# Perceiver layer on one core: the order of the first loads, keys, latents and maxima

## The chip, the cores and the metric

The kernel runs on one core of a Trainium2 chip. The metric is the device time of one execution in microseconds, as the median of several runs on the chip. The engines are TensorE (PE, with its weight loads shown apart as PEld), VectorE (DVE), ScalarE (ACT), GpSimd (POOL) and SyncE (SP); SP, ACT and POOL also issue DMAs, each through its own queue.

## What is computed

One layer with three residual blocks on latents x of 4 batches x 256 rows x 256: cross attention to a context of 4096 rows per batch, causal linear attention over the latents, and a gated feed-forward block. All is in float32. The change lies in the start of the first block:

```python
def _L0_xattn_ref(query, key, value, Wq, bq, Wk, bk, Wv, bv, Wh, bh):
    Q = query @ Wq.T + bq
    K = key @ Wk.T + bk
    V = value @ Wv.T + bv
    ...
    dot = jnp.einsum('bhsd,bhtd->bhst', Q, K) / np.sqrt(D_HEAD)
    scores = jax.nn.softmax(dot, axis=-1)
    out = jnp.einsum('bhst,bhtd->bhsd', scores, V)
    return out @ Wh.T + bh

x = x + _L0_xattn_ref(_layernorm(x), ctx_1024, ctx_1024, Wq, bq, Wk, bk, Wv, bv, Wh, bh)   # 16 heads of 16
x = x + _L0_attn_ref(_layernorm(x), ...)
x = x + _L0_ffn_ref(_layernorm(x), ...)
```

## The kernel before

**Tiling.** Cross attention runs in 16 units u, each one batch and four heads (`NU`), and each unit in 16 steps of 256 context rows (`NS`). A unit needs the keys of its heads for all 4096 context rows in one of three key buffers `kts`, and the largest score of each query row and head before its exponentials. The maxima of unit u + 1 are therefore made during the steps of unit u. The context comes in eight chunks of 512 rows (`NCH`), four chunk buffers (`cpool`), each chunk loaded by SP.

**Keys** (`key`, L630). For a chunk, 16 matmuls in two halves (tile `pk`), each evicted by ScalarE with the bias `bk_sb` into `ku` (L650), and after the second half eight DMAs (L653) that bring each head's rows into `kts`. For chunk 0 of the first batch the DMAs are issued by SP and ScalarE in turn, for all others by SP alone. The bias `bk_sb` is filled by sixteen small DMAs that GpSimd issues at the very start (L74), eight for each of its two columns. The weights arrive as `wk` and are copied without their padding to `wk_sb` (L883), on ScalarE.

**Latents and queries** (`queries`, L830). For a batch: `layernorm` (L96) in three pieces, statistics on VectorE, the root on ScalarE (L109), scaling on VectorE (L114); `turn`, which transposes on TensorE (L160) and copies to `zT` on ScalarE (L161); and `project`, queries of two head groups (tile `pq`, L848), evicted by ScalarE with the bias `bq_sb` into `qT` (L853).

**Maxima** (`maxima`, L694). For a unit and step, four matmuls of 128 queries by 512 keys (tile `pm`, L708), and one reduction each on VectorE (L715). When a unit's are complete, `shift` reduces them to `neg` (L722), transposes that on TensorE (`pn`, L727) and adds it to the queries (`qa`, L731), from which the main loop's scores (L745) are made.

**Order.** Inside `manual_schedule` (L861) TensorE, ScalarE, VectorE and SP do their work in the order in which the program is written; nothing overtakes on an engine. All PSUM tiles come from one pool of eight banks (`bank`, L179). The prologue of the first unit is written out by hand: loads, first keys, first queries, then sixteen groups g. In each group the four products of step g's maxima, a piece of the normalisation of batches 2 and 3 if one is due (`parts`), the reductions, and then one piece of `fill_in`: the keys of a chunk, the queries of a later batch (with `turn` in the piece where they are first wanted), or the values of a chunk. After groups 4, 6, 8 and 12 ScalarE fills a quarter of the third key buffer (`filled`, L906). After the groups named in `extra` come two groups of maxima of unit 1, ahead of its turn. Then the main loop begins, in which two units' work is interleaved until the causal attention and the feed-forward block follow.

Its core in the code:

```python
            for g, piece in enumerate(fill_in):
                products, reduce = maxima(g, range(4))
                products()
                if g in parts:
                    parts[g]()
                reduce()
                ...
                piece()
                ...
                if g in extra:
                    products, reduce = maxima(NS + extra[g], range(4))
```

Of the kernel before, what the change touches and what calls it, by code (L numbers as in the profile page):

```python
# [12 lines left out]
F32 = mybir.dt.float32  # L13
# [7 lines left out]
P = 128  # L21
B, T, D = 4, 256, 256
S = 4096
H, HD = 16, 16
KC = D // P
NT = B * T // P
NQ = H // 4
# [12 lines left out]
def perceiver_layer(  # L40
# [5 lines left out]
    nc = tc.nc  # L46
    const = ctx.enter_context(tc.tile_pool(name="const", bufs=1))

    def load(src, shape, name, dtype=F32, queue=None, pool=const):
        t = pool.tile(shape, dtype, tag=name, name=name)  # L50
        (queue or nc.scalar).dma_start(out=t, in_=src)
        return t


    xr = const.tile([P, NT, D], F32, tag="xr", name="xr")

    def load_x(b):
        nc.sync.dma_start(
            out=xr[:, 2 * b : 2 * b + 2, :],
            in_=x[b * T : (b + 1) * T, :].rearrange("(t p) d -> p t d", p=P),  # L60
        )

    load_x(0)
    eps = const.tile([P, 1], F32, tag="eps", name="eps")
    nc.gpsimd.memset(eps, LN_EPS)
    ident = const.tile([P, P], F32, tag="ident", name="ident")
    make_identity(nc, ident)
    wq_sb = load(wqP, [P, KC, NQ * P], "wq_sb")
    bq_sb = load(bqP, [P, NQ], "bq_sb")
    bk_sb = const.tile([P, KC], F32, tag="bk_sb", name="bk_sb")  # L70
    for q in range(NQ):
        for j in range(4):
            h = 4 * (q % 2) + j
            nc.gpsimd.dma_start(  # L74
                out=bk_sb[h * HD : (h + 1) * HD, q // 2 : q // 2 + 1],
                in_=bkP[32 * j + 1 : 32 * j + 1 + HD, q : q + 1],
# [208 lines left out]
    def start_causal():  # L285
# [75 lines left out]
        return norms, [call(lambda pieces: [piece() for piece in pieces], pieces) for pieces in others]  # L361

    finish = cross_attention(
        tc, xr, load_x, load_rest, ctxT, wq_sb, bq_sb, wkP, bk_sb, wvP, eps, ident, layernorm, transposed,
        qT, kts, lnp, bank, rest, start_causal)
    wout_sb = rest[8]

# [6 lines left out]
    for i in (0, 2):  # L374
        nc.gpsimd.affine_select(
            out=mask[:, i, :], in_=mask[:, i, :], compare_op=ALU.is_ge, fill=0.0, base=0,
# [189 lines left out]
                piece()  # L566


def cross_attention(tc, xr, load_x, load_rest, ctxT, wq_sb, bq_sb, wkP, bk_sb, wvP, eps,
                    ident, layernorm, transposed, qT, kts, lnp, bank, rest, start_causal):  # L570


# [14 lines left out]
    nc = tc.nc  # L587
# [4 lines left out]
    with ExitStack() as st:  # L592
# [10 lines left out]
        wk_sb = big.tile([P, KC, D], F32, tag="wk_sb", name="wk_sb")  # L603
        wv_sb = big.tile([P, KC, D], F32, tag="wv_sb", name="wv_sb")
        wide = st.enter_context(tc.tile_pool(name="wide", bufs=1))
        wk = wide.tile([P, KC, H, 32], F32, tag="wk", name="wk")
# [13 lines left out]
        def load_context():  # L620
            for _, p, c in itertools.islice(loads, 1):
                t = cpool.tile([P, KC, CH], F32, tag="ctx", name="ctx")
                nc.sync.dma_start(out=t, in_=ctxT[p // 2, c])
                contexts.append(t)

        def context(p, c):
            load_context()
            return contexts.pop(0)

        def key(p, c, queues=(nc.sync, nc.sync)):  # L630

            m, x = p % 2, context(p, c)
            ku = upool.tile([P, CH], F32, tag="ku", name="ku")
            made = []

            def half(part):
                pk = bank([P, CH // 2], "pk")
                made.append(pk)
                cs = slice(part * (CH // 2), (part + 1) * (CH // 2))
                for k in range(KC):  # L640
                    for j in range(4):
                        nc.tensor.matmul(  # L642
                            pk[32 * j : 32 * j + 32, :],
                            lhsT=wk_sb[:, k, m * P + 32 * j : m * P + 32 * j + 32], rhs=x[:, k, cs],
                            start=k == 0, stop=k == KC - 1,
                        )

            def out(part):
                cs = slice(part * (CH // 2), (part + 1) * (CH // 2))
                nc.scalar.activation(ku[:, cs], made.pop(), AF.Identity, bias=bk_sb[:, m : m + 1])  # L650
                for h in range(8 if part == 1 else 0):
                    r0 = 32 * (h % 4) + 1
                    queues[h % 2].dma_start(  # L653
                        out=kts[(2 * p + h // 4) % 3][r0 : r0 + HD, c * CH : (c + 1) * CH],
                        in_=ku[h * HD : (h + 1) * HD, :],
                    )

            return half, out
# [27 lines left out]
        def whole(item):  # L686
            half, out = item
            for part in range(2):
                half(part)
                out(part)  # L690
# [139 lines left out]
        def queries(b):  # L830

            z = lnp.tile([P, 2, D], F32, tag="z1", name="z1", bufs=4)
            got = []

            def norm():
                return layernorm(lambda t: z[:, t % 2, :], (2 * b, 2 * b + 1))

            def turn():
                zT = lnp.tile([P, KC, T], F32, tag="zT1", name="zT1")
                got.append(zT)  # L840
                for i in range(2):
                    transposed(zT[:, :, i * P : (i + 1) * P], z[:, i, :])

            def project(q):
                ps = bank([P, 2, T], "pq")
                for i in range(2):
                    for k in range(KC):
                        nc.tensor.matmul(  # L848
                            ps[:, i, :], lhsT=wq_sb[:, k, (q + i) * P : (q + i + 1) * P],
                            rhs=got[0][:, k, :], start=k == 0, stop=k == KC - 1,  # L850
                        )
                for i in range(2):
                    nc.scalar.activation(  # L853
                        qT[:, q + i, b * T : (b + 1) * T], ps[:, i, :], AF.Identity,
                        bias=bq_sb[:, q + i : q + i + 1],
                    )

            return norm, turn, project

        both = (nc.sync, nc.scalar)  # L860
        with tc.manual_schedule(engines={ET.PE, ET.Activation, ET.DVE, ET.SP}):  # L861
            nc.sync.dma_start(out=wk, in_=wkP.rearrange("p k (h r) -> p k h r", r=32))
            for b in range(1, B):
                load_context()
                load_x(b)
            nc.sync.dma_start(out=wv, in_=wvP)

# [5 lines left out]
            def fill(kt, c0, c1, engine=nc.vector):  # L873
                engine.tensor_copy(kt[:, c0 * CH : c1 * CH], ones.to_broadcast([P, (c1 - c0) * CH]))

            qs = [queries(b) for b in range(B)]
            for i in range(2):
                fill(kts[i], 0, 2)
            normal = [q[0]() for q in qs]
            for piece in normal[0]:  # L880
                piece()
            for k in range(KC):
                nc.scalar.copy(  # L883
                    wk_sb[:, k, :].rearrange("p (h d) -> p h d", d=HD), wk[:, k, :, 1 : 1 + HD]
                )
            qs[0][1]()
            whole(key(0, 0, both))
            qs[0][2](0)
            whole(key(0, 1))
            for i in range(2):  # L890
# [18 lines left out]
            def keys(c):  # L909
                return lambda: whole(key(0, c))  # L910

            def values(c):
                return lambda: whole(value(0, c))

            def turned(b, c):
                def piece():
                    qs[b][1]()
                    qs[b][2](2 * c)

                return piece  # L920

            def queried(b, c):
                return lambda: qs[b][2](2 * c)

            fill_in = [
                keys(3), keys(4), turned(1, 0), queried(1, 1), keys(5), turned(2, 0), keys(6), queried(2, 1),
                keys(7), turned(3, 0), values(0), queried(3, 1), values(1), queried(0, 1), values(2), values(3),
            ]

            parts = dict(zip((1, 2, 3, 6, 7, 8), (*normal[2], *normal[3])))  # L930
            extra = {10: 0, 13: 1}
            for g, piece in enumerate(fill_in):
                products, reduce = maxima(g, range(4))
                products()
# [20 lines left out]
            for n in range(NU * NS + 1):  # L955
# [14 lines left out]
                if i < len(items) - NCH:  # L970
                    if half == 0:
                        what, p, c = items[i + NCH]
# [96 lines left out]
```

## Time and profile before

| what | value |
|---|---|
| median of 3 runs | 1228.5 us (1228.21 to 1228.61) |
| the profiled execution | 1229.02 us, span 1227.3 us |
| TensorE busy | 1193.0 us, 97% of the span |
| VectorE busy | 927.9 us, 76% |
| ScalarE busy | 673.0 us, 55% |
| GpSimd busy | 60.2 us, 5% |
| DMA, 2 to 14 us of the span | about 400 GB/s |
| GpSimd's bias DMAs, issue to landing | 2.8 to 6.9 us, median 5.0 |

The span is the time from the first to the last instruction of the profiled execution; the device time has some 1.7 us around it. A profile line of a timeline gives the start, the length, the engine, the program line, the operation with the tile it writes and the tile it reads, the count of merged instructions, and in brackets how long the engine was idle before it and what ended that. A float32 matmul appears as two records. TensorE's busy share counts time in which a matmul waits for its bank, so that a stretched group of matmuls, not a gap, is how a wait for PSUM looks.

### The profile page before, as it was taken

The page shows a single profiled execution, that of the slowest core. Times are in us where ns is not written, and L with a number is a line of the kernel's source. Part 1 is how long each engine was busy: PE and PEld are TensorE (multiplying, and loading weights), DVE is VectorE, ACT ScalarE, POOL GpSimd, SP SyncE. Part 2 cuts the span into 40 slices and gives each one's busy share as a digit, 9 for nine tenths or more (in the row PEclk, how much of TensorE's full clock was granted, in tenths as well). Part 3 has the DMA queues.
Part 4 walks back from the last instruction along what each step waited for, and adds up shares of the span by engine and source line. Part 5 has one row for each costly group of instructions (what it writes and reads, how often), then busy time and mean ns, then how long its engine had stood idle before and what let it go on. Part 6 is the DMA issues. An engine that isn't in the chain of part 4 may idle for free.

```text
span 1227.3 us, 42096 instructions
## 1 busy us (share of the span) xinstructions
PE 1193.0 (97%) x17712; PEld 807.0 (66%) x17712; DVE 927.9 (76%) x1823; ACT 673.0 (55%) x1394; POOL 60.2 (5%) x115
## 2 busy tenths in 40 slices
PE   7999999999999999999999999999999999959998
PEld 3566667666766676667666776677667755536777
DVE  6887777777777777777777777777788877577763
ACT  3456665566666655666656556655566546641311
POOL 4010000000000000000000000000001012120100
PEclk9999999999999999999999999999999999999999
DMA  6452331233123322332233213322232000020000
GB/s 208 135 192 67 101 114 56 80 105 106 64 79 89 116 71 63 103 119 72 60 102 106 86 58 91 103 90 73 86 105 91 5 1 4 2 80 1 10 9 18
DMA packets 57756, 95.78 MB, mean 78 GB/s; under 512 B 29024, under 2 KB 31712, under 8 KB 57568
## 3 DMA queue, kind: packets, MB, share of 16 engines
q1 hardware_dynamic: 56640, 92.44, 24.3%
q8 instruction: 140, 2.29, 0.8%
q10 hardware_dynamic: 416, 0.66, 0.2%
q14 instruction: 48, 0.39, 0.1%
q0 software_dynamic: 512, 0.00, 0.0%
HBM read 74.17 MB, written 1.05 MB: 61 GB/s over the span
## 4 chain that ended last, share of the span: by engine, by line
PE 92%; DVE 4%; ACT 1%; DMA 1%; issue 1%; SPq 0%; POOL 0%; DVEq 0%; ACTq 0%
PE pt L745 22%; PE pm L708 18%; PE pav L765 18%; PE pk L642 11%; PE pv L672 10%; PE pd L504 2%; PE pg L492 1%; PE pu L492 1%; PE pq L848 1%; PE pqk L211 1%; PE po L430 1%; PE pa L411 1%; PE py L823 1%; PE py L466 1%; DVE mx L715 1%; PE pf L275 1%
## 5 line engine op out<-in xcount | busy, mean ns | idle before, releaser
L715 DVE TENSOR_REDUCE mx<-pm 128x1 f32<-128x512 f32 x1024 | 635.6, 684 | 145.4 <-PE pm L708 145.3
L750 ACT ACTIVATE e<-pt 128x512 f32<-128x512 f32 x1024 | 529.2, 602 | 384.2 <-PE pm L708 359.6
L745 PE MATMUL pt<-qa,kt 32*128 32x256 f32 x4096 | 500.2, 388 | 1.3 <-DVE av L775 0.7
L708 PE MATMUL pm<-kt,qT 32*128 32x512 f32 x2048 | 494.6, 616 | 0.0
L745 PEld LDWEIGHTS pt<-qa,kt 32*128 32x128 f32 x4096 | 317.0, 184 | 117.2 <-ACT v L679 43.2
L765 PE MATMUL pav<-e,v 128*32 128x256 f32 x4096 | 269.8, 380 | 0.0
L708 PEld LDWEIGHTS pm<-kt,qT 32*128 32x128 f32 x2048 | 172.2, 184 | 15.5 <-issue 3.7
L765 PEld LDWEIGHTS pav<-e,v 128*32 128x32 f32 x4096 | 128.7, 110 | 73.9 <-ACT e L750 4.7
L775 DVE TENSOR_TENSOR av<-pav,av 128x256 f32<-128x256 f32 x240 | 101.7, 424 | 65.7 <-PE pav L765 65.4
L672 PE MATMUL pv<-wv_sb,ctx 128*32 128x128 f32 x4096 | 137.5, 276 | 0.0
L642 PE MATMUL pk<-ctx,wk_sb 128*32 128x256 f32 x2048 | 136.7, 388 | 0.0
L672 PEld LDWEIGHTS pv<-wv_sb,ctx 128*32 128x32 f32 x4096 | 104.2, 109 | 43.5 <-DVE mx L715 42.7
L642 PEld LDWEIGHTS pk<-ctx,wk_sb 128*32 128x32 f32 x2048 | 54.8, 110 | 67.1 <-DVE mx L715 39.0
L650 ACT ACTIVATE ku<-pk,bk_sb 128x256 f32<-128x256 f32 x128 | 63.2, 495 | 11.2 <-PE pk L642 9.9
L679 ACT COPY v<-pv 128x256 f32<-128x256 f32 x128 | 51.4, 402 | 9.9 <-PE pv L672 9.9
L802 POOL TENSOR_TENSOR on<-on,bv_sb 128x64 f32<-128x64 f32 x32 | 9.2, 308 | 820.5 <-DVE on L797 820.5
L421 DVE TENSOR_TENSOR at<-pa,mask 128x384 f32<-128x384 f32 x64 | 31.2, 550 | 7.0 <-PE pa L416 7.0
L282 ACT ACTIVATE kt<-kt,shift 128x512 f32<-128x512 f32 x32 | 22.4, 725 | 22.0 <-DVE kt L281 22.0
L281 DVE TENSOR_SCALAR kt<-pf,low,top 128x512 f32<-128x512 f32 x32 | 23.7, 803 | 3.9 <-PE pf L275 3.9
L492 PE MATMUL pg<-zT,wg 128*128 128x256 f32 x96 | 23.0, 382 | 0.7 <-ACT zT L484 0.7
L496 ACT ACTIVATE th<-pg 128x512 f32<-128x512 f32 x12 | 7.1, 594 | 29.8 <-PE pg L492 29.8
L492 PE MATMUL pu<-zT,wu 128*128 128x256 f32 x96 | 22.7, 379 | 0.0
(126 smaller groups left out, 565.6 us busy)
## 6 DMA issues: line engine op xcount, KB each, us to landing
ctx<-in_ctxT_dram SPq DMA_DIRECT2D x128, 512.0 KB
kt<-ku SPq DMA_DIRECT2D x508, 32.0 KB
xo<-on SPq DMA_DIRECT2D x128, 8.0 KB
xr<-in_x_dram SPq DMA_DIRECT2D x4, 256.0 KB
out_dram<-o SPq DMA_DIRECT2D x8, 128.0 KB
wqkv_sb<-in_wqkv_dram SPq DMA_DIRECT2D x1, 768.0 KB
w_i<-in_w_gate_dram SPq DMA_DIRECT2D x1, 768.0 KB
w_i<-in_w_up_dram SPq DMA_DIRECT2D x1, 768.0 KB
```

The source lines that it names most:

```text
L421: nc.vector.tensor_tensor(at, pa, mask, ALU.mult)
L492: nc.tensor.matmul(ps[:, i, :], lhsT=w[:, k, ns], rhs=zT[:, k, :], start=k == 0, stop=k == KC - 1)
L642: nc.tensor.matmul(pk[32 * j : 32 * j + 32, :], lhsT=wk_sb[:, k, m * P + 32 * j : m * P + 32 * j + 32], rhs=x[:, k, cs], start=k == 0, sto ...
L650: nc.scalar.activation(ku[:, cs], made.pop(), AF.Identity, bias=bk_sb[:, m : m + 1])
L672: nc.tensor.matmul(pv[32 * j : 32 * j + 32, i, :], lhsT=x[:, k, t0 + 32 * j : t0 + 32 * j + 32], rhs=wv_sb[:, k, m * P : (m + 1) * P], sta ...
L679: nc.scalar.copy(to.rearrange("p t (h d) -> p t h d", d=HD + 1)[:, :, :, :HD], made.pop().rearrange("p t (h d) -> p t h d", d=HD),)
L708: nc.tensor.matmul(pm, lhsT=qT[rows, q, t0 : t0 + P], rhs=kt[rows, c * CH : (c + 1) * CH], start=True, stop=True,)
L715: nc.vector.tensor_reduce(mx[:, i, j, c : c + 1], pm, AX.X, ALU.max)
L745: nc.tensor.matmul(pt[:, i, :], lhsT=kt[rows, ks], rhs=qa[rows, :], start=True, stop=True)
L750: nc.scalar.activation(e, pt, AF.Exp, scale=0.25)
L765: nc.tensor.matmul(pav[32 * h : 32 * h + 32, :], lhsT=v[:, t % KT, c0 : c0 + 32], rhs=es[n, h][:, i, :], start=i == 0, stop=i == 1,)
L775: nc.vector.tensor_tensor(avs[u], pav, avs[u], ALU.add)
```

## The change

The first load of the latents no longer stands at the head of the program; `wq_sb` is only allocated there, and both are loaded by SP behind the key weights and the first context chunk. One of the two copies to `wk_sb` goes to VectorE. The keys of chunk 0 are made before the first normalisation. `turned`, which transposed a batch's latents and projected them in the same piece, becomes `ahead`, which puts the transposition behind the keys of an earlier piece; the projections stay where they were. The two groups of unit 1's maxima move from behind groups 10 and 13 to behind groups 4 and 9.

```diff
-    load_x(0)
     eps = const.tile([P, 1], F32, tag="eps", name="eps")
...
-    wq_sb = load(wqP, [P, KC, NQ * P], "wq_sb")
+    wq_sb = const.tile([P, KC, NQ * P], F32, tag="wq_sb", name="wq_sb")
     bq_sb = load(bqP, [P, NQ], "bq_sb")
...
             nc.sync.dma_start(out=wk, in_=wkP.rearrange("p k (h r) -> p k h r", r=32))
+            load_context()
+            load_x(0)
+            nc.sync.dma_start(out=wq_sb, in_=wqP)
             for b in range(1, B):
-                load_context()
+                if b < B - 1:
+                    load_context()
                 load_x(b)
             nc.sync.dma_start(out=wv, in_=wvP)
...
             for i in range(2):
                 fill(kts[i], 0, 2)
+            for k, copy in enumerate((nc.scalar.copy, nc.vector.tensor_copy)):
+                copy(wk_sb[:, k, :].rearrange("p (h d) -> p h d", d=HD), wk[:, k, :, 1 : 1 + HD])
+            whole(key(0, 0, both))
             normal = [q[0]() for q in qs]
             for piece in normal[0]:
                 piece()
-            for k in range(KC):
-                nc.scalar.copy(
-                    wk_sb[:, k, :].rearrange("p (h d) -> p h d", d=HD), wk[:, k, :, 1 : 1 + HD]
-                )
             qs[0][1]()
-            whole(key(0, 0, both))
             qs[0][2](0)
             whole(key(0, 1))
...
-            def turned(b, c):
-                def piece():
-                    qs[b][1]()
-                    qs[b][2](2 * c)
-
-                return piece
+            def ahead(piece, b):
+
+                return lambda: (piece(), qs[b][1]())
...
             fill_in = [
-                keys(3), keys(4), turned(1, 0), queried(1, 1), keys(5), turned(2, 0), keys(6), queried(2, 1),
-                keys(7), turned(3, 0), values(0), queried(3, 1), values(1), queried(0, 1), values(2), values(3),
+                keys(3), ahead(keys(4), 1), queried(1, 0), queried(1, 1), ahead(keys(5), 2), queried(2, 0),
+                keys(6), queried(2, 1), ahead(keys(7), 3), queried(3, 0), values(0), queried(3, 1),
+                values(1), queried(0, 1), values(2), values(3),
             ]

             parts = dict(zip((1, 2, 3, 6, 7, 8), (*normal[2], *normal[3])))
-            extra = {10: 0, 13: 1}
+            extra = {4: 0, 9: 1}
```

More of the change, by code (lines that the diff above doesn't have):

```diff
@@ L363, in perceiver_layer @@
     finish = cross_attention(
-        tc, xr, load_x, load_rest, ctxT, wq_sb, bq_sb, wkP, bk_sb, wvP, eps, ident, layernorm, transposed,
+        tc, xr, load_x, load_rest, ctxT, wqP, wq_sb, bq_sb, wkP, bk_sb, wvP, eps, ident, layernorm, transposed,
         qT, kts, lnp, bank, rest, start_causal)
@@ L566, in perceiver_layer, with cross_attention @@
                 piece()
-def cross_attention(tc, xr, load_x, load_rest, ctxT, wq_sb, bq_sb, wkP, bk_sb, wvP, eps,
+def cross_attention(tc, xr, load_x, load_rest, ctxT, wqP, wq_sb, bq_sb, wkP, bk_sb, wvP, eps,
                     ident, layernorm, transposed, qT, kts, lnp, bank, rest, start_causal):
```

## The prediction

> **What bounds the kernel now.** I read the page first: its chain of what ended last gives the kernel to TensorE. So any microsecond by which TensorE reaches its main loop later, or sooner, should show in full at the end.
>
> ```profile
> PE 92%; DVE 4%; ACT 1%; DMA 1%; issue 1%; SPq 0%; POOL 0%; DVEq 0%; ACTq 0%
> ```
>
> The change lies in the first 75 us, so I read the chain in order of time there (start, length, what), which gives the milestones to compare with.
>
> ```profile
> 0.81 4.59 DMA xr<-in_x_dram
> ...
> 7.71 1.09 PE tr L160 x4
> 8.80 3.38 PE pk L642 x32
> 12.19 1.93 PE pq L848 x8
> 14.11 3.59 PE pk L642 x64
> 17.70 1.07 PE pm L708 x8
> ...
> 65.37 7.26 DVE mx L715 x12
> 72.65 0.23 DVE neg L722
> 73.02 0.42 PE pn L727 x2
> ```
>
> Latents land first, TensorE starts at 7.71 us, the first group of maxima starts at 17.63 us (the timeline's start of that pm) and the last transposition before the main loop at 73.02. Note that the first keys take 3.38 us, the next two pieces together 3.59.
>
> Then the timeline of the first 32 us (start, length, engine, line; in brackets the idle time before and who ended it).
>
> ```profile
> 1.39 0.70 POOL L74 DMA_DIRECT2D bk_sb<-in_bkP_dram  x1 [0.35 <-issue]
> 2.44 3.61 POOL L74 DMA_DIRECT2D bk_sb<-in_bkP_dram  x7
> 6.62 0.30 ACT L109 ACTIVATE ln_rs<-ln_mv,eps 128x2 f32<-128x2 f32 x1 [3.31 <-DVE ln_mv L106]
> 10.73 0.47 ACT L650 ACTIVATE ku<-pk,bk_sb 128x256 f32<-128x256 f32 x1 [1.52 <-PE pk L642]
> 12.27 0.47 ACT L650 ACTIVATE ku<-pk,bk_sb 128x256 f32<-128x256 f32 x1 [1.06 <-PE pk L642]
> 12.77 2.50 ACTq L653 DMA_DIRECT2D kt<-ku  x4
> 15.38 0.84 ACT L853 ACTIVATE qT<-pq,bq_sb 128x256 f32<-128x256 f32 x2 [2.64 <-DMA kt<-ku]
> ```
>
> Two things to see. ScalarE issues half of the first keys' DMAs and does nothing else for 2.50 us: the queries, done at 14.1, are evicted only at 15.38. And the keys' bias bk_sb comes over GpSimd's queue: the first eight of sixteen transfers (column 0, all that the first keys read) are issued by 6.05; the eighth, from about 5.58, lands 4.9 us later (the DMA view), at 10.5. GpSimd's ninth issue starts 0.3 us after the landing it waits for, so a waiter would go at about 10.75. The first eviction started at 10.73, 0.30 us after its products' last issue (8.73 + half of 3.39 = 10.43); the second, which has its bias, 0.15 after its own (12.12). So the bias is just in time now.
>
> Last the loop's timeline.
>
> ```profile
> 55.09 9.72 DVE L715 TENSOR_REDUCE mx<-pm 128x1 f32<-128x512 f32 x16 [0.47 <-PE pm L708]
> 57.78 1.56 PE L708 MATMUL pm<-kt,qT 32*128 32x512 f32 x8
> 68.12 2.08 PE L708 MATMUL pm<-kt,qT 32*128 32x512 f32 x8
> ```
>
> A pm group (x8) normally takes 1.07; these two take 1.50 and 2.02. All PSUM tiles share eight banks in turn. Group 12's fourth pm is the eighth tile after group 11's first, which VectorE frees with its fifth reduction: 55.09 + 5 x 0.605 = 58.12; it can start at 58.21, and 58.21 + 1.07 = 59.28 is where the next matmul starts. Group 15: 65.35 + 6 x 0.605 + 0.09 = 69.07, + 1.07 = 70.14, again the trace's number. So I can tell by hand where TensorE will wait for a bank.
>
> [...] 0.43 us per four matmuls of the first keys against 0.23 later, full speed from 12.1, 4.4 us after the start. [...]
>
> **The change, the front.** Loads: wk, context 0, latents 0, wq, now all on SP's queue, where the latents led and wq ran on ScalarE's. By the DMA view 0.51 MB had moved by 4.0 us, 1.02 by 5.25, 1.31 by 6.0; the latents' 0.26 MB were in at 4.72 and used at 5.42, 0.70 later. So: wk (0.52 MB) usable at 4.7, its two copies, now one each on ScalarE and VectorE (0.40 each), done at 5.1; context at 6.0; latents at 6.7; wq at 8.0. TensorE starts the first keys at 6.0, cold as before: halves done at 7.7 and 9.4. That is 2.7 us earlier than now. SP issues the latents third instead of first and wq besides (0.44 to 0.5 us each, all four out by 2.8): hidden behind the 400 GB/s that set the landings; with ScalarE one issue short, its table load comes 0.5 earlier, into idle time. VectorE's wk copy fits between its fills (done 4.05) and the latents (6.7).
>
> But program order now puts on ScalarE: both evictions, four DMA issues, and only then the root of the first normalisation, without which there are no latents to transpose. The bias transfers do not move (same queue, same traffic): column 0 still lands at 10.5. So
>
> - evictions from 10.73, two in 0.84: done 11.57
> - four issues, 2.50 plus the gaps of now: root at 14.21
> - root to first transposition, as now 6.62 to 7.71: 15.30
> - transpositions and zT copies, cold: now 7.71 to 9.21, plus 0.07: queries from 16.87 (warm, as at 24.64 to 25.81: 16.5)
> - queries 1.93, keys 1 and 2 3.59: 22.4
>
> TensorE is idle from 9.4 to 15.3, 5.9 us. [...] Costed from both sides: no cold phase, first group at 16.5 + 5.52 = 22.0[...]. I take the 4.4 us of now, cold to 19.7: half of 19.7 - 16.87 is lost, 1.42, so the first maxima start at 23.8. **Front: 23.8 - 17.63 = +6.2 us.** VectorE's fills, memsets and second normalisation come behind this root too: from 15.7, 3.4 + 1.3 + 1.2 to 21.8, its root on ScalarE behind key 1's evictions (22.6), scaling done at 23.9. The first reduction is due at 24.96, so that cover holds by 1 us; gone, it would cost what it lacks. SP's key DMAs (8 x 0.69) start just as long before their group as now.
>
> **The loop.** Removed: three waits for zT between transposition and queries (24.70 + 0.38 to 25.81: 0.73 each, 2.2 us), as the transposition now sits one group ahead, with a pm group to hide the copy. Moved: two groups of unit 1's maxima (1.07 us TensorE, 2.42 VectorE each) from behind groups 10 and 13 to behind 4 and 9. There VectorE already has the four normalisation parts (1.08 and 0.92 twice each) and little slack. From the first group's start as zero, with pm 1.07, keys 1.87, queries 1.93, values 1.89, transposition 0.45, reductions 0.605 from 1.16 behind their group, I follow both engines and the eight banks:
>
> - group 2, ready 6.33: its fourth bank is group 1's fourth, reduced late since normalisation 2 precedes it: 7.15. Wait 0.82
> - extra group at 16.54 behind group 4: bank at 16.82. Wait 0.28
> - group 7, ready 23.83: bank of group 6's second, 24.92. Wait 1.09
> - group 9, ready 31.31: bank 31.89. Wait 0.58
> - group 11, ready 38.92: bank 39.77. Wait 0.85
> - group 15 starts at 51.69, its reductions clean of backlog, so the last transposition comes 1.15 + 2.48 + 0.40 = 4.03 later, at 55.72
>
> Now it is 73.02 - 17.63 = 55.39. The zT waits (2.2), the present bank waits (0.43 + 0.95) and their knock-on go; 3.6 us of new bank waits come. **Loop: +0.3 us.** Moving queued maxima and dropping the stall buys nothing: the late backlog of VectorE becomes an early one.
>
> Sum +6.5 us on the profiled execution's 1229.0 (span 1227.3 and 1.7 around it): 1235.5. The runs' median is 0.5 below that execution: **1235.0**, 0.5% slower.
>
> **Rivals.**
> - Clock stays up across the gap: front +4.4, total +4.7: 1233.2. Against it 5.9 us of idling.
> - The bias lands by 7.6: evictions follow the products (done 10.0), root 12.65, idle 4.3 and still cold: first group at 22.25, total +4.9: 1233.4. Late bias transfers landed in 3 to 3.8 us, but with less traffic.
> - Banks don't hold (the reading of eight in turn is wrong at the new places): loop -3.3, total +2.9: 1231.4. Against it two places reckoned to 0.01 us.
> - Not slower: ScalarE reaches the root early. Place: its queue between first eviction and root; price 4.2 us of the front. If the bias is there and the four issues cost ScalarE nothing, root at 10.05, queries at 12.3[...]: first group at 17.85, total +0.5: 1229.0. It decides from a root before about 10.5. Without the bank waits on top 1225.4, faster. The trace's 2.64 us wait speaks against it.
>
> **Numbers.** Chances: forecast 0.45, warm clock 0.17, early bias 0.13, no bank waits 0.13, early root 0.12 (0.05 of it with the second piece). A measurement of this kernel tells 0.2%, 2.5 us, from no change: slower above 1231.0. The no-bank-waits case lies near the bound, 0.05 of it under: slower 0.83, same 0.12, faster 0.05. Range 1231.0 to 1236.8: [...] the forecast's own range is 1234.3 to 1236.4.
>
> **What would show it.** Right: first keys on TensorE at about 6, first eviction near 10.7 with idle ScalarE before it, root near 14.2, transpositions near 15.3, no matmul from 9.4 until then, queries over 3 us long; first maxima at 22 to 25; stretched pm groups at 2, 7, 9 and 11. Wrong: a root near 10, a first group before 20, or a loop under 53 us.

## The result and the profile after

The changed kernel takes 1234.66 us in the median (1233.92 to 1235.62, 4 runs) beside 1228.55 before (1228.21 to 1228.62): a ratio of 1.0051, 95% interval 1.0033 to 1.0068. It is slower by 0.5%, 6.1 us; 1235.0 was forecast. One execution each of e5, e10 and e11 below took at least 275 us longer than the others of its kernel, and these three are not in the ratios.

The chain by engine of the changed kernel's page is again TensorE's, over a longer span.

```profile
span 1232.2 us, 42099 instructions
...
PE 92%; DVE 4%; DMA 1%; ACT 1%; issue 1%; SPq 0%; POOL 0%; ACTq 0%; DVEq 0%
```

Its timeline of the first 40 us, the columns as before (start, length, engine, line, what; idle before it and by whom ended):

```profile
5.95 3.64 PE L641 MATMUL pk<-ctx,wk_sb 128*32 128x256 f32 x32 [5.95 <-DMA ctx<-in_ctxT_dram]
...
10.71 0.84 ACT L649 ACTIVATE ku<-pk,bk_sb 128x256 f32<-128x256 f32 x2 [5.80 <-DMA bk_sb<-in_bkP_dram]
...
11.59 2.75 ACTq L652 DMA_DIRECT2D kt<-ku  x4
14.39 0.30 ACT L108 ACTIVATE ln_rs<-ln_mv,eps 128x2 f32<-128x2 f32 x1 [2.83 <-DMA wv<-in_wvP_dram]
...
15.48 1.08 PE L159 MATMUL tr<-ident,z 128*128 128x128 f32 x4 [5.88 <-DVE z L113]
...
17.02 3.42 PE L847 MATMUL pq<-zT,wq_sb 128*128 128x256 f32 x8 [0.46 <-ACT zT L160]
...
20.37 3.66 PE L641 MATMUL pk<-ctx,wk_sb 128*32 128x256 f32 x64
...
23.96 1.14 PE L707 MATMUL pm<-kt,qT 32*128 32x512 f32 x8
```

TensorE starts 1.8 us earlier (5.95 instead of 7.71) and reaches the first maxima 6.3 us later. The first keys wait on ScalarE for their bias until 10.71, the root waits behind them and four DMA issues until 14.39, and TensorE idles 5.88 us. Then the queries take 3.35 us to the next start (17.02 to 20.37) instead of 1.92 (12.12 to 14.04 before). The length shown, 3.42, is 0.07 more; below, a length of a group of matmuls is the time to the next start.

The granted TensorE clock says why. In the windows of the changed kernel each row gives the busy time of PE, PEld, DVE, ACT and POOL, then the clock as a share of full speed, the DMA share and GB/s.

```profile
10.00:12.00 2.00, 0.00 (x0) 0.00 (x0) 0.00 (x0) 0.84 (x2) 2.00 (x5) 1.00 1.03 376
12.00:14.00 2.00, 0.00 (x0) 0.00 (x0) 0.00 (x0) 0.00 (x0) 1.50 (x1) 0.78 1.07 415
14.00:16.00 2.00, 0.52 (x3) 0.55 (x4) 1.25 (x4) 0.30 (x1) 0.00 (x0) 0.50 0.51 148
...
18.00:20.00 2.00, 2.00 (x6) 1.60 (x5) 1.79 (x4) 0.00 (x0) 0.00 (x0) 0.51 0.42 170
20.00:22.00 2.00, 2.00 (x34) 1.07 (x37) 1.47 (x6) 1.32 (x3) 0.00 (x0) 1.00 0.00 0
```

It halves near 13.1 (0.78 over two microseconds is half speed for the last 0.9 of them) and returns near 19.95. Over the 3.35 us of the queries its mean is 0.56, which is 1.88 us at full speed, about the 1.92 that they take in the kernel before. (The column reads 1.00 for the first keys too. That they run at half speed is read from their length alone: the timeline shows them with 3.64 us at 5.95, and as many products at 25.04 with 1.93.)

In TensorE's timeline of the loop the stretched pm groups are now early; a pm group normally takes 1.07.

```profile
30.42 1.80 PE L707 MATMUL pm<-kt,qT 32*128 32x512 f32 x8
...
47.81 2.25 PE L707 MATMUL pm<-kt,qT 32*128 32x512 f32 x8
...
55.43 1.45 PE L707 MATMUL pm<-kt,qT 32*128 32x512 f32 x8
...
62.67 2.08 PE L707 MATMUL pm<-kt,qT 32*128 32x512 f32 x8
...
79.56 0.41 PE L726 MATMUL pn<-ident,neg 128*128 128x128 f32 x2 [1.02 <-DVE neg L721]
```

These are groups 2, 7, 9 and 11. From the first maxima to the last transposition it is 55.60 us; before, 55.39. At 79.56 the changed kernel is 6.54 us behind.

This difference holds to the last unit's maxima (`neg`, last at 1006.6 before, 1013.1 after), but the first tanh of the feed-forward block comes only 4.9 us later (1121.5, 1126.4). Between them the clock falls in both kernels, at other moments. The windows of before, then of after:

```profile
1084.00:1086.00 2.00, 2.00 (x18) 1.33 (x17) 0.66 (x3) 0.00 (x0) 0.00 (x0) 0.50 0.67 172
```

```profile
1092.00:1094.00 2.00, 2.00 (x19) 1.08 (x20) 2.00 (x4) 1.49 (x3) 0.48 (x1) 0.50 0.67 277
```

Before, half speed lay over features (line 275); after, a piece later, over attention products (line 410) that have a wait behind them. So 1.6 us of the 6.5 are gone again at the end of this pair of profiled executions. The other profiles speak against the change as the reason: from the last transposition of the prologue to the end of the span, thirteen profiled executions (all of this document but e5's) take between 1151.9 and 1154.8 us, and the kernels with the new front (1151.9 to 1154.8) do not differ from those with the old one (1152.2 to 1154.3). The kernel before is near the top with 1154.3, the changed one near the middle with 1152.6. That it is the clock's timing is read from these windows and was not tested.

### The profile page after: what moved, and what is told of

Its sections match the earlier page's. It is cut to its first block, busy times and chain, and to the rows that moved or that the text cites. A ratio compares the mean times of both kernels' runs of the same rounds, so it can differ in the third digit from the quotient of the medians.

```text
span 1232.2 us, 42099 instructions
## 1 busy us (share of the span) xinstructions
PE 1196.4 (97%) x17712; PEld 809.8 (66%) x17712; DVE 928.2 (75%) x1824; ACT 672.6 (55%) x1393; POOL 57.4 (5%) x115
## 4 chain that ended last, share of the span: by engine, by line
PE 92%; DVE 4%; DMA 1%; ACT 1%; issue 1%; SPq 0%; POOL 0%; ACTq 0%; DVEq 0%
PE pt L744 22%; PE pm L707 19%; PE pav L764 18%; PE pv L671 10%; PE pk L641 10%; PE pd L503 2%; PE pg L491 1%; PE pu L491 1%; PE pq L847 1%; PE pqk L210 1%; PE po L429 1%; PE pa L410 1%; PE py L822 1%; PE py L465 1%; DMA wv<-in_wvP_dram 1%
```

## The experiments

Totals of one kernel vary (39 runs of the kernel before on the chip of e11: 1227.08 to 1229.39 us, at mean granted clocks of 0.993 to 0.998), so beside the ratio to the kernel before (with its interval) I read two milestones: the start of the first maxima, and the length from there to the last transposition ("loop"), both from the one profiled execution of each kernel.

**e1: the first keys' DMAs all on SP.**

```diff
-            whole(key(0, 0, both))
+            whole(key(0, 0))
```

> The changed kernel with all eight DMAs of the first keys on SP, none on ScalarE. Theory (ScalarE's four issues stand between the second eviction and the root): the root moves from 14.4 to 11.7 us, the first transposition to 12.75, queries from about 14.1; [...] first maxima at 19.5 (full clock) to 21.3 (half clock again) instead of 23.96, total 1230.2 to 1232.0. Rival (the loads or the order on TensorE set the front, the issues are hidden): first maxima stay at 24, total 1234.7.

1234.24 us, ratio 1.0046 (1.0030 to 1.0063); first maxima 23.04, a miss by 1.7. The root did move to 11.67, but its gain was mostly lost behind it, as the timeline shows:

```profile
11.84 2.04 POOL L298 MEMSET va<- 128x2304 f32 x1
...
12.20 2.14 DVE L113 TENSOR_SCALAR z<-xr,ln_mv,ln_rs 128x256 f32<-128x256 f32 x2
...
14.17 1.08 PE L159 MATMUL tr<-ident,z 128*128 128x128 f32 x4 [4.61 <-DVE z L113]
```

The two scalings took 2.14 us instead of 0.74: they fell onto GpSimd's fill of `va`. At the usual length, and with the end at 14.34 that they had, they would have begun at 13.60, near the end of the fill at 13.88. That the fill delayed them is read from these times and was not tested alone. Then the queries took 3.71 us, as at half clock. So the issues do delay the root (2.7 us, as expected), but only a third of it (0.9) reached the maxima, and the total is nearer to the rival's.

**e2: the bias in one DMA.** The host lays it out; GpSimd issues none.

```diff
-    bk_sb = const.tile([P, KC], F32, tag="bk_sb", name="bk_sb")
-    ...
+    bk_sb = load(bkP, [P, KC], "bk_sb")
...
-        "bkP": _heads_apart(p["xattn_bk"], True).reshape(NQ, P).T,
+        "bkP": p["xattn_bk"].reshape(KC, P).T,
```

> The changed kernel with the keys' bias laid out on the host and loaded by one DMA on ScalarE's queue instead of sixteen on GpSimd's. Theory (the bias gates the first eviction): evictions at 7.8 and 9.5 instead of 10.7, issues from 10.0, root at 12.85, idle TensorE 9.4 to 13.9 and cold again, first maxima at 22.4 (20.6 if the clock stays up), total about 1233.1. Rival (the first eviction waits for something else, or the issues alone decide): first eviction stays near 10.7 and the first maxima at 24.

1235.12 us, 1.0055 (1.0039 to 1.0070); first maxima 23.67, a miss by 1.3. The evictions came earlier (the second at 10.41), though the context came 0.8 later (first keys from 6.72), and why is open. But the root did not:

```profile
10.41 0.47 ACT L642 ACTIVATE ku<-pk,bk_sb 128x256 f32<-128x256 f32 x1 [1.23 <-PE pk L634]
...
10.92 3.53 ACTq L645 DMA_DIRECT2D kt<-ku  x4
14.50 0.29 ACT L101 ACTIVATE ln_rs<-ln_mv,eps 128x2 f32<-128x2 f32 x1 [3.61 <-DMA wv<-in_wvP_dram]
```

The issues are not dearer (0.51 to 0.60 each); the fourth starts only at 13.94, and in the changed kernel at 13.82; in both, the profile puts the end of ScalarE's wait down to the landing of `wv`, a load that the keys do not use. Behind the bias stands a second wait that ends at almost the same time: ScalarE's last issue for that load. Why it waits for it is in the last section.

**e3: both edits.** 

> Both edits. Theory: the two costs add along one chain: root at 10.1, transposition 11.2, queries near 12.5, first maxima at 17.9 (full clock) to 19.6 (half clock again), total 1228.7 to 1230.3: the front is then level with the kernel before, which shows that nothing else in the new order costs. Rival (loads set the front): first maxima no earlier than with the better one of the two edits alone.

1230.07 us, 1.0014 (1.0005 to 1.0022); first maxima 19.84.

```profile
10.46 0.29 ACT L101 ACTIVATE ln_rs<-ln_mv,eps 128x2 f32<-128x2 f32 x1
...
11.54 0.67 PE L152 MATMUL tr<-ident,z 128*128 128x128 f32 x4 [1.51 <-DVE z L106]
...
12.68 3.63 PE L840 MATMUL pq<-zT,wq_sb 128*128 128x256 f32 x8 [0.47 <-ACT zT L153]
```

Alone the edits gave 0.9 and 0.3 us, together 4.1: each removes one of two waits side by side. (The expected range ended at 19.6.) With both gone the first maxima are 2.2 us behind the kernel before. Of that, 1.65 is the clock, which fell behind a gap of 1.51 us (queries 3.57 instead of 1.92); the other 0.6 is less than the 0.9 by which the context came later, as in e2.

**e4: TensorE kept busy.** 40 matmuls without a reader behind the first keys; the computation of the layer is unchanged.

```diff
             whole(key(0, 0, both))
+            spin = bank([P, CH // 2], "spin")
+            for r in range(5):
+                for k in range(KC):
+                    for j in range(4):
+                        nc.tensor.matmul(
+                            spin[32 * j : 32 * j + 32, :], lhsT=wk_sb[:, k, 32 * j : 32 * j + 32],
+                            rhs=wk_sb[:, k, :], start=k == 0, stop=k == KC - 1,
+                        )
```

> The changed kernel with 40 matmuls that nobody reads, behind the first keys, so that TensorE is busy from 9.4 to about 15.5 us. Theory (the idle stretch costs half the clock): queries last 1.9 to 2.0 us instead of 3.42, first maxima at 22.0 instead of 23.96, total 1232.7. Rival (the queries are slow for another reason, weights or operands arriving late): they still last over 3 us and the first maxima come at 24 or later.

1233.31 us, 1.0041 (1.0026 to 1.0056); first maxima 24.01, queries 3.51 us: by the expectation's letter the rival won. The windows around them say otherwise:

```profile
15.00:16.00 1.00, 0.23 (x2) 0.20 (x3) 0.96 (x4) 0.00 (x0) 0.00 (x0) 1.00 0.26 62
16.00:16.50 0.50, 0.43 (x4) 0.20 (x2) 0.50 (x1) 0.29 (x2) 0.00 (x0) 1.00 0.01 4
16.50:17.00 0.50, 0.09 (x1) 0.09 (x1) 0.50 (x1) 0.36 (x2) 0.00 (x0) 0.74 0.00 0
17.00:17.50 0.50, 0.50 (x1) 0.41 (x2) 0.50 (x1) 0.00 (x0) 0.00 (x0) 0.50 0.27 66
```

The filler ended at 14.05; full clock still at the transposition, half from about 16.75. TensorE still had gaps of 1.71 us ahead of the transposition and of 0.48 behind it.

**e5 and e12: kept busy without gaps.** 56 matmuls there and 8 between the transposition and the queries.

> The changed kernel with 56 matmuls that nobody reads behind the first keys and 8 more between the first transposition and the queries, so that TensorE has neither the gap of 1.7 us nor most of the 0.5 us that the filler of 40 left. Theory[...]: queries at 16.9 to 17.2 last 1.93 instead of 3.42 to 3.58, first maxima at 22.4 instead of 23.96. Rival (the queries are slow after any filler, for their operands): over 3 us again, first maxima at 24.

The ratio is 1.0041 (1.0027 to 1.0055). The profile is of the one long execution, with a mean clock of 0.75, and says nothing on the queries. So once more, for its profile:

> The kernel of e5 once more, for a profile in which the granted clock is not the lower one of that run. Theory: at full clock the queries take 1.93 us from about 17.1, first maxima at 22.4 to 22.7. Rival: over 3 us, 24.

1234.81 us in one run. Its timeline:

```profile
16.78 0.66 PE L159 MATMUL tr<-ident,z 128*128 128x128 f32 x4
17.37 1.07 PE L901 MATMUL spin<-wk_sb 128*32 128x256 f32 x16
18.37 1.99 PE L847 MATMUL pq<-zT,wq_sb 128*128 128x256 f32 x8
...
20.29 3.66 PE L641 MATMUL pk<-ctx,wk_sb 128*32 128x256 f32 x64
```

The queries take 1.92 us: same operands, full clock (1.00 in every window from 9 to 22 us). So the clock made them slow, by 1.43 us. First maxima still at 23.89, a miss by 1.2, since the filler overran: it held the transposition to 16.78 and the queries to 18.37, 1.35 later than without. The mechanism is shown; the saving was not obtained this way.

**e6, e7, e8: the loop's two edits apart.** e6 is the changed kernel, e7 the kernel before, each with the other's `extra` (the diff is e6's; e7's is its reverse); e8 is the kernel before with `ahead`.

```diff
-            extra = {4: 0, 9: 1}
+            extra = {10: 0, 13: 1}
```

> The changed kernel with unit 1's two groups of maxima behind groups 10 and 13 again. Theory (eight banks in turn, followed by hand as in the prediction): waits of 0.82 before group 2, 0.28 at 5, 0.62 at 9, 0.2 at 12, 0.85 at 15; from the first maxima to the last transposition 54.85 us instead of 55.60, total 0.75 lower. Rival (the early place is what relieves VectorE at the end, as VectorE bounds the last groups): over 56 us.

> The kernel before with unit 1's two groups of maxima behind groups 4 and 9, nothing else. Theory (bank by bank): the late waits at 12 and 15 go, new ones of 0.25 at 6 and 0.85 at 11 come, first maxima to last transposition 55.4 us as before (55.39), total 1228.5 within 0.3. Rival (VectorE's end is relieved and nothing is paid earlier): 54.5 or less, total about 1227.5.

> The kernel before with the transpositions a group ahead of their queries, nothing else. Theory: three waits of 0.73 go, but the transposition's two banks and the faster run bring waits for VectorE at 2, 5, 9, 12 and 15: 54.85 us from the first maxima to the last transposition instead of 55.39, total 0.5 lower, 1228.0. Rival (the waits for zT are simply saved): 53.2 us, total about 1226.3.

| kernel | transposition | groups behind | loop reckoned, us | loop measured, us | ratio |
|---|---|---|---|---|---|
| before | with its queries | 10, 13 | | 55.39 | |
| e7 | with its queries | 4, 9 | 55.4 | 55.46 | 0.9996 (0.9987 to 1.0005) |
| e8 | ahead | 10, 13 | 54.85 | 54.68 | 0.9987 (0.9980 to 0.9993) |
| e6 | ahead | 10, 13 | 54.85 | 54.68 | 1.0049 (1.0034 to 1.0064) |
| after | ahead | 4, 9 | 55.72 | 55.60 | 1.0051 (1.0033 to 1.0068) |

The banks reckoned by hand hit all four loops within 0.2 us. `ahead` is worth 0.7 us; moving the groups to 4 and 9 costs 0.9 with it and nothing without. e6's total does not show its gain. In its profiled execution the front was 0.8 us later (first maxima 24.78, queries 3.71, as wholly at half clock); whether that holds for its other three runs is not known.

**e9: root first.** The changed kernel, with the first keys' evictions and DMAs behind the copies to zT. (The lines behind the first dots make an eviction take the older of two waiting halves.)

```diff
...
-            whole(key(0, 0, both))
+            first = key(0, 0, both)
+            for part in range(2):
+                first[0](part)
             normal = [q[0]() for q in qs]
             for piece in normal[0]:
                 piece()
             qs[0][1]()
+            for part in range(2):
+                first[1](part)
             qs[0][2](0)
```

> The changed kernel with one order changed: root, scaling and the copies to zT stand before the evictions of the first keys, so neither the bias nor ScalarE's four issues are ahead of the root. Loads, bias and issues are as they were. Theory (the order on ScalarE alone makes the front late): root at 7.8, first transposition at 9.4, queries from 10.9, first maxima at 16.5 to 18.3 instead of 23.96, total 1227.5 to 1229.5. Rival (bias and issues hold the front in any order, as the queries' eviction is behind them too): first maxima after 20.

1228.54 us, 0.9999 (0.9990 to 1.0007); first maxima 18.43, loop 55.58.

```profile
7.90 0.30 ACT L108 ACTIVATE ln_rs<-ln_mv,eps 128x2 f32<-128x2 f32 x1 [3.11 <-DVE ln_mv L105]
...
10.05 0.80 ACT L160 COPY zT<-tr 128x256 f32<-128x256 f32 x2 [1.86 <-PE tr L159]
...
11.05 0.84 ACT L649 ACTIVATE ku<-pk,bk_sb 128x256 f32<-128x256 f32 x2 [0.20 <-DMA bk_sb<-in_bkP_dram]
```

Bias, issues and loads are as late as ever, and 5.5 of the 6.3 us are gone: the loss was the order on ScalarE. What is left, 0.8 us, is less than what half clock costs the queries (3.72 us, 1.8 more than at full clock).

**e10: no gap on TensorE, groups behind 8 and 12.** As e9, with key chunk 1's products between transposition and queries.

> The order of e9, with the products of key chunk 1 between the transposition and the queries so that TensorE has no gap, and the two groups of unit 1's maxima behind groups 8 and 12, where reckoning bank by bank gives the shortest loop, 54.0 us. Theory: first maxima at 15.6 to 17.3, last transposition near 70.5 (73.02 before), total 1226.0, faster than both. Rival (something else of the new order costs): first maxima no earlier than 17.6.

0.9999 (0.9991 to 1.0007), so not faster as expected. TensorE was done with keys and queries at 15.8, the queries at full clock again (1.92 us), but

```profile
17.97 1.73 PE L707 MATMUL pm<-kt,qT 32*128 32x512 f32 x8 [2.17 <-DMA kt<-ku]
```

the maxima wait for the first keys' rows. Their DMAs are issued from 11.78 on, behind the bias, and the maxima start 6.2 us after that; in the kernel before it was 4.9 us (12.77 to 17.63), without a wait. So the next bound is the way of these rows; how much of it is the late bias and how much the transfer beside the loads was not separated. Behind this gap of 2.17 us keys 3 take 3.35 us (19.62 to 22.97) instead of 1.87, as at half clock. That lies in the loop, which is 55.44 us where 54.0 was reckoned, so that the last transposition, at 73.41, is 0.4 behind the kernel before.

**e11: the kernel before with `ahead` and groups behind 8 and 12.** 

> The kernel before with the transpositions a group ahead and the two groups of maxima behind 8 and 12. Theory (bank by bank): 54.0 us from first maxima to last transposition instead of 54.68 with 10 and 13, total 0.7 below that one (1227.3), 1226.6. Rival (the place of the groups does not matter once the zT waits are gone): 54.7 us.

0.9986 (0.9979 to 0.9992); median 1226.47 beside 1228.0 of the kernel before on the same chip.

```profile
18.64 1.14 PE L708 MATMUL pm<-kt,qT 32*128 32x512 f32 x8
...
72.36 0.41 PE L727 MATMUL pn<-ident,neg 128*128 128x128 f32 x2 [0.99 <-DVE neg L722]
```

The loop is 53.72 us, 0.28 under the reckoning and 0.96 under e8's. With e8 it beats both kernels; the intervals of the two do not part them.

## Why the prediction was right

Step by step, forecast against the profiled execution: first keys 6.0 (5.95), first eviction 10.73 (10.71), root 14.21 (14.39), transposition 15.30 (15.48), queries from 16.87 (17.02), first maxima 23.8 (23.96), loop +0.3 (+0.2), sum +6.5 (+6.54 at the last transposition; the median +6.1).

- **The order on ScalarE** was the cause: e9 undoes it alone and regains 5.5 us.
- **Bias and issues.** Both terms came out, the issues with some luck: they took 2.75 us for the 2.50 forecast, since the fourth waited 0.35 for `wv`, which was not foreseen. And the rival "the bias lands early" was priced wrong: it assumed the issues take 2.5 us whenever they start. In e2 they took 3.53, the fourth waiting for `wv` until 13.9, so an early bias alone is worth 0.3 us, not 1.6. The two waits overlap, and only removing both shows (e3).
- **The clock**: 1.42 us forecast, 1.43 measured on the queries, and shown by e12. That the clock would be down behind the gap, and for the 4.4 us of the kernel's start, was an estimate; it came back 4.5 us after the transposition's start (15.48 to 19.95). The kernel before shows the fall too, near 1084 us and near 1104, behind idle stretches of 3.6 and 3.8 us, which the page's tenths hide.
- **The loop.** Bank waits of 0.67, 0.27, 1.11, 0.32 and 0.95 us at groups 2, 6, 7, 9 and 11, 3.3 in all, for the 3.6 reckoned; the one foreseen ahead of the extra group did not come, one at 6 did. e6 to e8 and e11 carry the mechanism to other placings; e10, where half clock fell into the loop, missed its length by 1.4 us.
- The 1.6 us that the profiled execution gained back late in the kernel was not forecast: it took 1233.9 where 1235.5 had been reckoned for it. That the median came within 0.4 us of 1235.0 is therefore partly luck, as the rest of the kernel varies by up to 2.9 us from one profiled execution to another.

## What to carry to other kernels

Starting an engine earlier gains nothing if the work put first has a tail, evictions and DMA issues, on another engine that works in program order and that the next step needs (here a start 1.8 us earlier, and first maxima 6.3 us later): follow each moved step through every queue it is issued on. With a fixed ring of PSUM banks, write down which reduction frees the bank of each product; that gave five loop lengths to 0.3 us, wherever the clock stayed up, and the better placing. And look for a second wait close behind the one removed.

## What the runs showed of the hardware

- TensorE's clock fell behind gaps of different length. In the changed kernel it halved near 13.1, within the gap of 5.88 us. In e4 it halved near 16.75, behind gaps of 1.71 and 0.48 us; from the end of the filler (14.05) up to then TensorE was busy for 0.67 us, the transpositions. In e3 the gap was 1.51 us, and the queries from 12.68 on took 3.57 us instead of 1.92; in e10 it was 2.17 us, and keys 3 took 3.35 instead of 1.87. But in the kernel before a gap of 2.57 us, up to 1092.02, left the clock at 1.00 (every window from 1088 to 1100 us), so the length of the one gap does not decide it. How little work lets the clock fall cannot be read from these runs.
- A DMA issue can wait for an earlier DMA that it shares no data with, and on ScalarE the compute behind it then waits too: in e2 the third and fourth of four waited 0.4 and 0.8 us. The waits in the changed kernel show which one it is. Counted over SP and ScalarE together, in the order of their starts, the ninth DMA (latents of batch 2) waited 0.4 us for the first (`bq_sb`), the eleventh (`wv`) 0.2 us for the third (context chunk 0), the twelfth (chunk 3) 0.4 us for the fourth (latents of batch 0), and ScalarE's last key issue, the nineteenth, 0.35 us for the eleventh, `wv`. Each waits for the one issued eight earlier. So in this program it is a matter of order and count, and not of `wv` being a large load: the load eight places ahead decided how long each of these issues was held.
- In the kernel before GpSimd's small DMAs took 4.9 to 5.5 us from issue to landing beside the loads (the first nine; all DMAs together moved 373 GB/s in the mean from 2 to 14 us), the tenth 6.9, and the last six 2.8 to 3.8, which run past the loads' end (about 100 GB/s from 15 us on).
